# Two attention layers on one core: group totals in pairs, differences of the next input on GpSimd, and broadcasts placed within the even steps

## The chip, the cores and the metric

The kernel runs on one core of a Trainium2 chip. The metric is device time in microseconds, the median of several runs. The time before is 3956.3 us (three runs, 3953.38 to 3957.62).

A core has five engines with a queue each: TensorE (PE, matrix products), VectorE (DVE), ScalarE (ACT), GpSimd (POOL) and SyncE (SP, which here only issues DMAs; GpSimd issues some too). Each engine works its queue in order, and waits for the others by semaphores.

## The reference, cut to what matters

The input x has 8 images of 512 channels and 32 x 32 = 1024 positions. Two layers follow one another, both with 8 heads of 64 channels, all in float32:

```python
# layer 0, on gn(x): group norm, then plain attention
weight = softmax(einsum('bct,bcs->bts', q * s, k * s))      # 1024 x 1024 for each head
a = einsum('bts,bcs->bct', weight, v)
x = x + einsum('oc,bct->bot', proj_w, xf + a) + proj_b
# layer 1, on gn(x): attention with mixed heads, and an instance norm of the weights
attn = einsum('bhdq,bhdT->bhqT', q, k) * scale
attn = softmax(einsum('gh,bhqT->bgqT', w_head, attn))
attn = (attn - mean) / sqrt(var + EPS) * in_gamma + in_beta  # over each head's 1024 x 1024
out = einsum('bhqT,bhdT->bhqd', attn, v) @ w_proj.T + b_proj
x = x + out
```

What matters here: both softmaxes are left undivided until after the product with v. The kernel forms exponentials, sums of them (the totals), reciprocals of the totals, and multiplies the attention's output with the reciprocals, which it must first spread over the partitions by way of DRAM.

## The kernel before

**Projections.** Every 512 x 512 projection is a 2 x 2 block product by 7 products instead of 8 (Winograd's form of Strassen). It needs sums and differences of the four quarters of the right-hand side: `combine_right` forms four differences, each of 128 x 1024 elements, the second from the first and the fourth from the second. `ORDER = (1, 6, 2, 7, 5, 3, 4)` is one order of the products. Product 6 needs the second difference, product 7 the third, product 5 the first and product 4 the fourth; 1, 2 and 3 need none.

**Layer 0, attention** (`attention0`, once per batch). The work is 64 pieces, i = 0 to 63, eight per group g; a group is a pair of heads and half of the positions. `scores(i)` makes 1024 scores per partition on PE and exponentials on ACT; `values(i)` multiplies them with v on PE; `sums(i)` adds the exponentials into `zacc[g]` on DVE. The loop takes two pieces at a time, with values two pieces behind the scores. What else is due stands in an agenda by slot (a value of i): with i the end of a group, `totals(g)` at i + 2, `reciprocals(g)` at i + 6, `finish(g)` at i + 10.

- `totals(g)`: four small matmuls with a matrix of ones sum `zacc[g]` over the partitions into a PSUM tile z, 256 columns in each of four 32-row strips. ACT copies it to `row`, SP stores it into `zc[g]` by DMA as 128 x 8.
- `reciprocals(g)`: DVE adds the two halves of the output, takes the reciprocal, SP writes it to DRAM (`zd`) and reads it back spread over 64 partitions, twice (`rzb[g]`); two small checks follow on DVE.
- `finish(g)`: DVE multiplies the output with `rzb[g]` and adds it into `xa`.

What is due after slot 65 runs in a flush, `ag.flush()`, that stands behind the next batch's first projection (`qk0`, or `first_q1` after the last batch) and before its second (`v0`, or `first_k1`). During the attention the agenda also holds the statistics of the next batch (`stats0`: slots 20 to 47, with two small matmuls pm and pv at slots 43 and 45 that PE executes in order between its pieces) and loads: `load_left("k")` at 32, `load_left("v")` at 33, 1792 KB each.

**Layer 1, attention** (`Attention1`, once per batch). The positions of the queries are taken in 8 chunks p, with each step in four quarters t. Chunk p's scores are made in step p, moved by DMA so that a head lies on its own partitions (`regroup`, `re<-raw`), mixed over the heads on PE and exponentiated on ACT in step p + 1 (`mix`), transposed on DVE (`flip`), measured on DVE (`moments`, the BN statistics), and multiplied with v in steps p + 1 and p + 2 (`values`). Step 8 has no new chunk: it is the turn, where the first projection of the next batch (`k_projection`, its right-hand side the next input y) is woven in. `right_tile` takes a tile from the pool of the raw scores, `right_y` fills it with the four differences of y, and `k_go(1)`, `(2)`, `(6)`, `(7)`, later `(5)` and `(4, 3)`, are the products. Each product's result leaves PSUM by `leave`, on DVE or ACT, and the PSUM pool has three such tiles, shared with the scores and the mix.

Two chunks make a pair n. `totals(n)` stands in the second quarter of the odd steps (p = 3, 5, 7): DVE takes reciprocals, GpSimd writes them to DRAM in four DMAs (`zd<-rz`) and reads them back spread over 64 partitions each, in two DMAs (`rzb<-zd`, `broadcast(0)` and `broadcast(1)`), and `divide` on GpSimd multiplies the output with them (`q<-q,rzb`) in the last quarter of the even steps. The last pair of a batch does the same after step 8 on SP and DVE.

**What sets the order.** No scheduler reorders anything: each engine's queue holds its instructions in the order in which the program text emits them, by the steps and the agendas. A tile's pool hands out its buffers in that order too, and an instruction waits where its buffer is still in use.

Of the kernel before, what the change touches and what calls it, by code (L numbers as in the profile page):

```python
# [9 lines left out]
F32 = mybir.dt.float32  # L10
# [8 lines left out]
P = 128  # L19
# [448 lines left out]
def tile_two_attention_layers(  # L468
# [19 lines left out]
    nc = tc.nc  # L488
    B, C, T = x_d.shape
# [3 lines left out]
    NT = T // P  # L493
    FB = 512
# [206 lines left out]
    with ExitStack() as l0:  # L701
# [49 lines left out]
        def load_blocks(which, queue=nc.sync, tag="u0"):  # L751

            t = left_tile(which, 0)
            if tag == "junk":
                a21[which] = zpool.tile([P, T], F32, tag=tag, name=f"a21_{which}", bufs=1)[
                    :, :C
                ].rearrange("p (k o) -> p k o", k=2)
            else:
                a21[which] = zpool.tile([P, 2, HC], F32, tag=tag, name=f"a21_{which}")
            for dst, i, j in (  # L760
                (t[:, 0], 0, 0), (t[:, 1], 0, 1), (a21[which], 1, 0), (t[:, 2], 1, 1),
            ):
                for k in range(2):
                    queue.dma_start(
                        out=dst[:, k],
                        in_=SOURCES[which][ts(2 * j + k, P), i * HC : (i + 1) * HC],
                    )
# [308 lines left out]
        def attention0(b, agenda):  # L1076
# [18 lines left out]
            def sums(i):  # L1095
                g, kc = i // NG, i % NG
                if kc == 1:
                    zacc[g] = zpool.tile([P, 2, FB], F32, tag="zacc", name=f"zacc_{b}_{g}")
                    nc.vector.tensor_add(zacc[g], e[i - 1], e[i])  # L1099
                elif kc > 1:  # L1100
                    nc.vector.tensor_add(zacc[g], zacc[g], e[i])  # L1101

            def values(i):

                g, hp, kc = i // NG, i // NG % (H // 2), i % NG
                if kc == 0:
                    acc[g] = [
                        ps_a.tile([P, FB], F32, tag=f"a{a}", name=f"a0_{b}_{g}_{a}", bufs=2 - a)
                        for a in range(2)
                    ]  # L1110
                for a in range(2):
                    rows = slice(a * D, a * D + D)
                    for m in range(2):
                        nc.tensor.matmul(  # L1114
                            acc[g][a][m * D : m * D + D], v[rows, kc, ts(2 * hp + m, D)],
                            e[i][rows, m], start=(kc == 0), stop=(kc == NG - 1),
                        )
                if kc == NG - 1:

                    u[g] = [  # L1120
                        zpool.tile([P, FB], F32, tag=f"u{a}", name=f"u_{b}_{g}_{a}")
                        for a in range(2)
                    ]
                    for a in (1, 0):
                        nc.scalar.copy(u[g][a], acc[g][a])

            def totals(g):


                HB = FB // 2  # L1130
                z = ps_a.tile([P, FB], F32, tag="a0", name=f"z_{b}_{g}", bufs=2)[:, :HB]
                for c in range(4):
                    nc.tensor.matmul(
                        z[c * 32 : c * 32 + 32], ones[:, :32], zacc[g][:, c // 2, ts(c % 2, HB)],
                        start=True, stop=True, tile_position=(0, c * 32),
                    )
                row = zpool.tile([P, HB], F32, tag="row", name=f"row0_{b}_{g}")
                nc.scalar.copy(row, z)
                zc[g] = stat.tile([P, T // P], F32, tag="zc", name=f"zc_{b}_{g}")
                nc.sync.dma_start(out=zc[g], in_=row[0::32])  # L1140

            def reciprocals(g):

# [22 lines left out]
            def finish(g):  # L1166
                hp, f = g % (H // 2), g // (H // 2)
                nc.vector.tensor_mul(u[g][0], u[g][0], rzb[g])
                dst = xa_t[b][:, hp, ts(f, FB)]
                nc.vector.tensor_add(dst, dst, u[g][0])  # L1170


            for i in range(0, NI + 2, 2):
                if i < NI:
                    scores(i)
                    scores(i + 1)
                if i >= 2:
                    for w in (i - 2, i - 1):
                        values(w)
                        sums(w)  # L1180
                    if (i - 1) % NG == NG - 1:
                        g = (i - 1) // NG
                        agenda.at(i + 2, lambda g=g: totals(g))
                        agenda.at(i + 6, lambda g=g: reciprocals(g))
                        agenda.at(i + 10, lambda g=g: finish(g))
                agenda.run(i)
                agenda.run(i + 1)

# [82 lines left out]
    with ExitStack() as l1:  # L1271
# [78 lines left out]
        def quarters(n):  # L1350
            return [[n[:, 2 * i : 2 * i + 2, ts(j, FB)] for j in range(2)] for i in range(2)]

        def combine_right(t, n, parts=range(4)):

            (b11, b12), (b21, b22) = quarters(n)
            for i in parts:
                x, y = ((b12, b11), (b22, t[:, 0]), (b22, b12), (b21, t[:, 1]))[i]
                nc.vector.tensor_sub(t[:, i], x, y)  # L1358

        class Projection:  # L1360
            ORDER = (1, 6, 2, 7, 5, 3, 4)
# [63 lines left out]
            t = rawpool.tile([P, H * FB], F32, tag="raw", name=f"left_p_{b}")  # L1425
            load_left(("p", b), t[:, : 14 * HC])

        def right_y(b, parts=range(4)):
            combine_right(right_t[b], y_t[b], parts)

        def k_projection(b):
            t = k_t[b] = shared.tile([P, NCC, T], F32, tag="k", name=f"k1_{b}")
# [192 lines left out]
        class Attention1:  # L1625
# [140 lines left out]
            def totals(self, n):  # L1766

                b, last = self.b, n == NCH - 1
                bn = self.stats(n)
                del self.bn[n]  # L1770
                ps = acc_psum(f"z1_{b}_{n}")
                nc.tensor.matmul(ps[:64, :32], bn[:, :, 1], sel256, start=True, stop=True)
                for i, x in enumerate((bn[:, :, 2], self.sq)):
                    nc.tensor.matmul(ps[:64, 32:64], x, sel, start=(i == 0), stop=(i == 1))
                rz = stat.tile([64, 32], F32, tag="rz", name=f"rz1_{b}_{n}")
                nc.vector.reciprocal(rz, ps[:64, :32])  # L1776
                nc.vector.tensor_copy(self.zs[:, n], ps[:64, :64])
                zd = dram.tile([2, H, P], F32, tag=f"zd_{b}_{n}", name=f"zd_{b}_{n}")
                queue = nc.sync if last else nc.gpsimd
                for r in range(2):  # L1780
                    for t in range(2):
                        queue.dma_start(  # L1782
                            out=zd[t].rearrange("g (r c q) -> r c g q", r=2, q=4)[r],
                            in_=rz[32 * t + r : 32 * t + 32 : 2].rearrange("c (g q) -> c g q", q=4),
                        )
                self.rzb = zpool.tile([P, T], F32, tag="rzb", name=f"rzb_{b}_{n}")
                self.zd, self.zq = zd, queue
                self.broadcast(0)

            def broadcast(self, t):  # L1790

                self.zq.dma_start(
                    out=self.rzb[t * D : t * D + D],
                    in_=self.zd[t].rearrange("g i -> (g i)").partition_broadcast(D),
                )
# [70 lines left out]
            def step(self, p, t, ag):  # L1866

                new, old, older = p < NT, p >= 1, p >= 2
                if t == 0:
# [10 lines left out]
                    if old:  # L1880
                        self.mix(p - 1, 0)
                    ag.run(4 * p - 0.25)
                elif t == 1:
                    if older:
                        self.values(p - 2, 1, 0)
                        self.flip(p - 1, 0)
                        if p % 2:
                            self.totals(p // 2 - 1)
                        elif p >= 4:
                            self.broadcast(1)  # L1890
                        self.moments(p - 1, 0)
                    if new:
                        self.scores(p, 3)
# [2 lines left out]
                    if old:  # L1896
                        self.mix(p - 1, 1)
                elif t == 2:
                    if older:
                        self.values(p - 2, 1, 1)  # L1900
                    if new:
# [63 lines left out]
        for b in range(B):  # L1965
# [11 lines left out]
            if more:  # L1977
# [14 lines left out]
                kp = []  # L1992
                ag.at(4 * NT - 0.5, lambda: right_tile(b + 1))
                ag.at(4 * NT - 0.5, lambda: k_go(1))
                ag.at(4 * NT, lambda: right_y(b + 1, [0, 1]))
                ag.at(4 * NT + 0.5, lambda: k_go(2))
                ag.at(4 * NT + 1, lambda: right_y(b + 1, [2, 3]))
                ag.at(4 * NT + 1, lambda: left_p(b))
                ag.at(4 * NT + 1.5, lambda: k_go(6))
                ag.at(4 * NT + 2.5, lambda: k_go(7))  # L2000
# [16 lines left out]
            if not more:  # L2017
                a.values(last, 0, 2, 3)
                a.leave(last, 0)
                out_products[0](0, [2])  # L2020
                out_products[0](1, [0, 1])
                a.values(last, 1, 0, 1, 2, 3)
                a.leave(last, 1)
                a.totals(NCH - 1)
                a.broadcast(1)
                a.instance()
                out_products[1]()
                continue
# [4 lines left out]
            a.values(last, 1, 0, 1, 2, 3)  # L2033
            a.leave(last, 1)
            a.totals(NCH - 1)
            a.broadcast(1)
            a.instance()
            k_leave()
# [72 lines left out]
```

## Time and profile before

| what | us |
|---|---|
| median of three runs | 3956.3 |
| the profiled execution's own time | 3957.8 |
| its span, first to last instruction | 3956.0 |
| PE busy in it | 3873.6 |
| the four small matmuls of totals in layer 0, L1133, all 64 groups | 40.9 |
| the copy of z on ACT, L1138, 64 of 0.37 | 23.8 |
| differences of y on DVE, L1358 `right`, 28 of 1.21 (median) | 33.8 |
| product with the reciprocals on GpSimd, L1819, 24 | 56.5 |

The granted TensorE clock was 0.999 over the whole span.

The sums of busy time are of overlapping pieces. A group's line in the profile gives line, engine, operation, output and input tiles with their shapes, how many, and then busy us and mean ns of one, and the idle time of the engine before them with what ended it. These are the two largest groups, one of layer 1 on DVE and one of layer 0 on PE:

```profile
L1704 DVE STREAM_TRANSPOSE et<-e 128x2048 f32<-128x2048 f32 x256 | 589.4, 2302 | 100.4 <-ACT e L1689 99.2
...
L1088 PE MATMUL s<-q,k 64*64 64x512 f32 x4096 | 490.1, 593 | 2.3 <-ACT e L1093 2.3
```

PE matmuls overlap, so that 593 ns is the length of one and not the distance to the next. A float32 matmul leaves two records. In the order of time, a line has the start, the length of the merged piece, the engine, the source line, the operation and, in brackets, the idle time before it and what released it.

### The profile page before, as it was taken

To read this page: it belongs to the slowest core of one execution; us is meant where nothing else is said; L and a number is where in the kernel's file an instruction comes from. 1 tells how busy PE (TensorE), PEld (TensorE's weight loads), DVE (VectorE), ACT (ScalarE), POOL (GpSimd) and SP (SyncE) were. 2 spreads that over 40 slices of the span, in tenths; PEclk is the share of its full clock that TensorE was granted. 3 is DMA by queue.
4 is the path that set the end of the run, shared out by engine and by line. 5 is a ranking of instruction groups with operands and counts; after the bars stand their busy time and mean duration, and the time that the engine had idled before them with its cause. 6 is when DMAs were issued, how large, how long until landed. Compare 5 with 4: busy or idle time off the path is not lost. (4 is left out here: it accounts for less than half of the span.)

```text
span 3956.0 us, 95453 instructions
## 1 busy us (share of the span) xinstructions
PE 3873.6 (98%) x41868; PEld 1820.5 (46%) x41868; DVE 2770.1 (70%) x3741; ACT 1970.7 (50%) x2432; POOL 140.9 (4%) x182
## 2 busy tenths in 40 slices
PE   8999999999999999999999999999999999999998
PEld 4353534344353535344544544545545445445454
DVE  4747475665758474756967958859768769678597
ACT  1726354453627172534816717538347257176274
POOL 0000000000000000000100100001001001001010
PEclk9999999999999999999999999999999999999999
DMA  3313131121122121216938839749558479297495
GB/s 120 123 49 116 49 118 38 63 69 68 55 72 68 62 76 49 86 46 170 233 120 202 217 100 236 191 125 241 161 148 220 144 178 237 83 231 197 117 226 143
DMA packets 249593, 519.09 MB, mean 131 GB/s; under 512 B 51024, under 2 KB 58192, under 8 KB 242512
## 3 DMA queue, kind: packets, MB, share of 16 engines
q1 hardware_dynamic: 241984, 500.08, 44.6%
q0 software_dynamic: 7184, 12.81, 1.6%
q8 instruction: 331, 5.42, 0.6%
q14 instruction: 94, 0.77, 0.1%
HBM read 197.16 MB, written 46.92 MB: 62 GB/s over the span
## 5 line engine op out<-in xcount | busy, mean ns | idle before, releaser
L1704 DVE STREAM_TRANSPOSE et<-e 128x2048 f32<-128x2048 f32 x256 | 589.4, 2302 | 100.4 <-ACT e L1689 99.2
L1734 PEld LDWEIGHTS a<-et,v 128*64 128x64 f32 x16384 | 506.0, 138 | 290.7 <-issue 263.6
L1718 DVE BATCH_NORM_STATS2 bn<-e 128x6 f32<-128x512 f32 x1024 | 634.9, 680 | 0.0
L1093 ACT ACTIVATE e<-s 128x1024 f32<-128x1024 f32 x512 | 497.2, 1026 | 234.2 <-PE s L1088 233.8
L1651 ACT COPY raw<-s 128x1024 f32<-128x1024 f32 x480 | 470.2, 1018 | 214.3 <-PE s L1639 189.6
L1689 ACT ACTIVATE e<-m 128x1024 f32<-128x1024 f32 x512 | 496.2, 1021 | 156.7 <-PE m L1676 54.9
L1734 PE MATMUL a<-et,v 128*64 128x64 f32 x16384 | 553.8, 224 | 6.1 <-issue 3.5
L1101 DVE TENSOR_TENSOR zacc<-zacc,e 128x1024 f32<-128x1024 f32 x384 | 468.7, 1221 | 88.4 <-ACT e L1093 66.3
L1639 PE MATMUL s<-k,q 64*64 64x512 f32 x4096 | 514.6, 606 | 5.9 <-DVE q L1498 3.2
L1088 PE MATMUL s<-q,k 64*64 64x512 f32 x4096 | 490.1, 593 | 2.3 <-ACT e L1093 2.3
L1114 PE MATMUL a<-e,v 64*64 64x512 f32 x4096 | 484.0, 589 | 0.0
L1676 PE MATMUL m<-re,wmix 32*32 32x512 f32 x8192 | 312.5, 599 | 19.6 <-DMA re<-raw 16.1
L1114 PEld LDWEIGHTS a<-e,v 64*64 64x64 f32 x4096 | 156.7, 133 | 282.8 <-issue 282.5
L1088 PEld LDWEIGHTS s<-q,k 64*64 64x64 f32 x4096 | 147.9, 133 | 275.1 <-issue 240.7
L1639 PEld LDWEIGHTS s<-k,q 64*64 64x64 f32 x4096 | 128.1, 132 | 220.6 <-issue 87.8
L1458 PE MATMUL pv<-wv,y 128*128 128x512 f32 x480 | 214.3, 599 | 0.0
L1782 POOL DMA_DIRECT2D zd<-rz x96 | 52.3, 550 | 3507.7 <-DVE rz L1776 3505.6
L1750 ACT COPY q<-a 64x256 f32<-64x256 f32 x256 | 93.9, 367 | 145.8 <-PE a L1734 144.2
L1676 PEld LDWEIGHTS m<-re,wmix 32*32 32x32 f32 x8192 | 69.3, 103 | 165.0 <-ACT raw L1651 74.6
L1458 PEld LDWEIGHTS pv<-wv,y 128*128 128x128 f32 x480 | 88.6, 190 | 119.8 <-issue 106.5
L1464 DVE COPY v<-pv 128x512 f32<-128x512 f32 x30 | 20.7, 689 | 159.6 <-PE pv L1458 81.0
L1099 DVE TENSOR_TENSOR zacc<-e,e 128x1024 f32<-128x1024 f32 x64 | 78.3, 1223 | 55.4 <-ACT e L1093 55.4
(318 smaller groups left out, 3871.0 us busy)
## 6 DMA issues: line engine op xcount, KB each, us to landing
re<-raw SPq DMA_DIRECT2D x1024, 256.0 KB
left_q<-left_q SPq DMA_DIRECT2D x17, 1792.0 KB
left_p<-left_p SPq DMA_DIRECT2D x17, 1792.0 KB
left_k<-left_k SPq DMA_DIRECT2D x10, 1792.0 KB
x<-in_x_dram SPq DMA_DIRECT2D x32, 512.0 KB
rzb<-zd SPq DMA_DIRECT2D x128, 128.0 KB
x<-x SPq DMA_DIRECT2D x64, 256.0 KB
y<-x SPq DMA_DIRECT2D x32, 512.0 KB
```

The source lines that it names most:

```text
L1088: nc.tensor.matmul(ps[c * D : c * D + D, m], k[r, hp, k0 : k0 + D], q[r, hp, ts(f, FB)], start=True, stop=True,)
L1093: nc.scalar.activation(e[i], ps, AF.Exp, scale=S0 * S0)
L1101: nc.vector.tensor_add(zacc[g], zacc[g], e[i])
L1114: nc.tensor.matmul(acc[g][a][m * D : m * D + D], v[rows, kc, ts(2 * hp + m, D)], e[i][rows, m], start=(kc == 0), stop=(kc == NG - 1),)
L1458: nc.tensor.matmul(ps[:, m], y_t[b][:, c, ts(2 * i + m, P)], w[:, c], start=(c == 0), stop=(c == NCC - 1),)
L1639: nc.tensor.matmul(ps[c * D : c * D + D, m], qo_t[b][r, p, hp, ts(c, D)], k_t[b][r, hp, ts(kh, FB)], start=True, stop=True,)
L1651: nc.scalar.copy(dst, ps)
L1676: nc.tensor.matmul(ps[a // 2][c * 32 : c * 32 + 32, a % 2].rearrange("p (r h k) -> p h r k", r=2, h=2), wmix[rows].rearrange("p g i -> p ( ...
L1689: nc.scalar.activation(e[:, :, 2 * h : 2 * h + 2].rearrange("p r a k -> p a r k"), ps[h].rearrange("p a (r k) -> p a r k", r=2), AF.Exp,)
L1704: nc.vector.transpose(self.et[p, u].rearrange("p kb (r st a) g q -> p st kb r (a g q)", r=2, st=2)[:, st], self.e[p, s].rearrange("p r a ( ...
L1718: nc.vector.bn_stats(self.bn[n][:, p % 2, s, a], e[:, :, a].rearrange("p r k -> p k r"))
L1734: nc.tensor.matmul(acc[two * D : two * D + D, s].rearrange("p (x q) -> p x q", q=4), v_t[b][:, kb, ts(g, D)], et[:, kb, :, g], start=(kb = ...
```

## The change

It has three parts.

1. **Layer 0.** `totals(g)` is called for odd g alone and handles g - 1 and g: eight small matmuls into one PSUM tile of 512 columns, one copy of 512 columns on ACT, two DMAs into `zc`. Its slot, two after the odd group's end, stays; `reciprocals` of both groups follow in one slot (i + 6), and `finish` of the two at i + 10 and i + 12. To hold two groups, `zacc`, the first half of the output `u0` and the tile `a21` that shares its tag get three buffers instead of two, `zc` four, and `row` one of double width.
2. **Layer 1, the turn.** `right_y` forms all four differences on GpSimd at one place, in the first quarter of step 8 before the mix, right after `right_tile`; before, DVE formed two at the end of the first quarter and two at the end of the second. `combine_right` gets the engine as an argument; the other call, for the output's projection, stays on DVE.
3. **Layer 1, broadcasts.** `totals(n)` no longer calls `broadcast(0)`. Both broadcasts stand in the even steps, the first at the end of the first quarter's mix, the second at the start of the third quarter; after step 8 they are called explicitly for the last pair, in the order as before. The tile `rzb` is taken when the first broadcast is issued.

```diff
             def totals(g):
                 HB = FB // 2
-                z = ps_a.tile([P, FB], F32, tag="a0", name=f"z_{b}_{g}", bufs=2)[:, :HB]
-                for c in range(4):
-                    nc.tensor.matmul(
-                        z[c * 32 : c * 32 + 32], ones[:, :32], zacc[g][:, c // 2, ts(c % 2, HB)],
-                        start=True, stop=True, tile_position=(0, c * 32),
+                z = ps_a.tile([P, FB], F32, tag="a0", name=f"z_{b}_{g}", bufs=2)
+                for i in range(2):
+                    for c in range(4):
+                        nc.tensor.matmul(
+                            z[c * 32 : c * 32 + 32, ts(i, HB)], ones[:, :32],
+                            zacc[g - 1 + i][:, c // 2, ts(c % 2, HB)],
+                            start=True, stop=True, tile_position=(0, c * 32),
+                        )
+                row = zpool.tile([P, FB], F32, tag="row", name=f"row0_{b}_{g}", bufs=1)
+                nc.scalar.copy(row, z)
+                for i in range(2):
+                    t = zc[g - 1 + i] = stat.tile(
+                        [P, T // P], F32, tag="zc", name=f"zc_{b}_{g - 1 + i}", bufs=4
                     )
-                row = zpool.tile([P, HB], F32, tag="row", name=f"row0_{b}_{g}")
-                nc.scalar.copy(row, z)
-                zc[g] = stat.tile([P, T // P], F32, tag="zc", name=f"zc_{b}_{g}")
-                nc.sync.dma_start(out=zc[g], in_=row[0::32])
+                    nc.sync.dma_start(out=t, in_=row[0::32, ts(i, HB)])
...
                         g = (i - 1) // NG
-                        agenda.at(i + 2, lambda g=g: totals(g))
-                        agenda.at(i + 6, lambda g=g: reciprocals(g))
-                        agenda.at(i + 10, lambda g=g: finish(g))
+                        if g % 2:
+                            agenda.at(i + 2, lambda g=g: totals(g))
+                            for j in range(2):
+                                agenda.at(i + 6, lambda g=g - 1 + j: reciprocals(g))
+                                agenda.at(i + 10 + 2 * j, lambda g=g - 1 + j: finish(g))
...
-        def right_y(b, parts=range(4)):
-            combine_right(right_t[b], y_t[b], parts)
+        def right_y(b):
+            combine_right(right_t[b], y_t[b], nc.gpsimd)
...
-                self.rzb = zpool.tile([P, T], F32, tag="rzb", name=f"rzb_{b}_{n}")
-                self.zd, self.zq = zd, queue
-                self.broadcast(0)
+                self.zd, self.zq, self.zn = zd, queue, n
 
             def broadcast(self, t):
 
+                if t == 0:
+                    self.rzb = zpool.tile(
+                        [P, T], F32, tag="rzb", name=f"rzb_{self.b}_{self.zn}"
+                    )
...
                     ag.run(4 * p - 0.25)
+                    if p % 2 == 0 and p >= 4:
+                        self.broadcast(0)
                 elif t == 1:
...
                         if p % 2:
                             self.totals(p // 2 - 1)
-                        elif p >= 4:
-                            self.broadcast(1)
...
                 elif t == 2:
+                    if p % 2 == 0 and p >= 4:
+                        self.broadcast(1)
...
                 ag.at(4 * NT - 0.5, lambda: right_tile(b + 1))
                 ag.at(4 * NT - 0.5, lambda: k_go(1))
-                ag.at(4 * NT, lambda: right_y(b + 1, [0, 1]))
+                ag.at(4 * NT - 0.5, lambda: right_y(b + 1))
                 ag.at(4 * NT + 0.5, lambda: k_go(2))
-                ag.at(4 * NT + 1, lambda: right_y(b + 1, [2, 3]))
```

More of the change, by code (lines that the diff above doesn't have):

```diff
@@ L758, in load_blocks @@
             else:
-                a21[which] = zpool.tile([P, 2, HC], F32, tag=tag, name=f"a21_{which}")
+                a21[which] = zpool.tile([P, 2, HC], F32, tag=tag, name=f"a21_{which}", bufs=3)
             for dst, i, j in (
@@ L1097, in sums @@
                 if kc == 1:
-                    zacc[g] = zpool.tile([P, 2, FB], F32, tag="zacc", name=f"zacc_{b}_{g}")
+                    zacc[g] = zpool.tile(
+                        [P, 2, FB], F32, tag="zacc", name=f"zacc_{b}_{g}", bufs=3
+                    )
                     nc.vector.tensor_add(zacc[g], e[i - 1], e[i])
@@ L1120, in values @@
                     u[g] = [
-                        zpool.tile([P, FB], F32, tag=f"u{a}", name=f"u_{b}_{g}_{a}")
+                        zpool.tile([P, FB], F32, tag=f"u{a}", name=f"u_{b}_{g}_{a}", bufs=3 - a)
                         for a in range(2)
@@ L1351, in quarters, with combine_right @@
             return [[n[:, 2 * i : 2 * i + 2, ts(j, FB)] for j in range(2)] for i in range(2)]
-        def combine_right(t, n, parts=range(4)):
+        def combine_right(t, n, engine=nc.vector):
             (b11, b12), (b21, b22) = quarters(n)
-            for i in parts:
+            for i in range(4):
                 x, y = ((b12, b11), (b22, t[:, 0]), (b22, b12), (b21, t[:, 1]))[i]
-                nc.vector.tensor_sub(t[:, i], x, y)
+                engine.tensor_sub(t[:, i], x, y)
         class Projection:
@@ L1785, in totals @@
                         )
-                self.rzb = zpool.tile([P, T], F32, tag="rzb", name=f"rzb_{b}_{n}")
-                self.zd, self.zq = zd, queue
-                self.broadcast(0)
+                self.zd, self.zq, self.zn = zd, queue, n
             def broadcast(self, t):
+                if t == 0:
+                    self.rzb = zpool.tile(
+                        [P, T], F32, tag="rzb", name=f"rzb_{self.b}_{self.zn}"
+                    )
                 self.zq.dma_start(
@@ L2024, in tile_two_attention_layers @@
                 a.totals(NCH - 1)
+                a.broadcast(0)
                 a.broadcast(1)
@@ L2035, in tile_two_attention_layers @@
             a.totals(NCH - 1)
+            a.broadcast(0)
             a.broadcast(1)
```

## The prediction

> **What bounds the kernel.** I read the page first, then what TensorE (PE) waits for, then the order of time at the places the diff touches.
>
> ```profile
> PE 3873.6 (98%) x41868; PEld 1820.5 (46%) x41868; DVE 2770.1 (70%) x3741; ACT 1970.7 (50%) x2432; POOL 140.9 (4%) x182
> ...
> PE pk L1383 <- DVE re L1400: 8.2, 7, 1.2
> ...
> PE pk L1383 <- DVE right L1358: 2.6, 7, 0.4
> ```
>
> The columns of a wait are total us, times, longest. PE is hardly ever idle, so the time falls by PE work taken out plus PE waits taken out; nothing else counts. Two of these waits come exactly 7 times, once for each turn from one batch to the next in layer 1.
>
> **Part 1, totals of two groups together.** PE in layer 0, in order of time:
>
> ```profile
> 1410.36 1.90 PE L1088 MATMUL s<-q,k 64*64 64x512 f32 x16
> 1412.08 1.90 PE L1114 MATMUL a<-e,v 64*64 64x512 f32 x16
> 1413.90 0.64 PE L1133 MATMUL z<-zacc,ones 128*32 128x256 f32 x8
> 1414.47 1.95 PE L1088 MATMUL s<-q,k 64*64 64x512 f32 x16
> 1416.24 1.90 PE L1114 MATMUL a<-e,v 64*64 64x512 f32 x16
> ```
>
> Without a z, pieces start every 1.72 us. From a (1412.08) to the next a (1416.24) is 4.16 us where two pieces are 3.43: a visit of z costs 0.73 us. What would a second group in the same visit cost? A 16-record piece is two rounds of four tiles side by side over 512 columns in 1.72, so 0.86 a round; z has 256 columns, so 0.43 (estimate). At worst it costs the 0.64 that the row shows as its whole span. I take 0.43, since nothing changes between the two rounds.
>
> Per batch there are 7 visits in the loop and one in the flush after it. Afterwards 3 remain in the loop and 1 in the flush, each with two groups. Removed: 4 x 0.73 = 2.92, but in 7 batches one removed z shares its visit with the small matmul pm of the statistics (z to pm takes 0.57), so there 2.75. Added: 3 x 0.43 = 1.29. In the flush PE now waits 0.28 for DVE after z (pv_p started 236.97, k ended 236.92), so the added 0.43 costs only 0.15. Sum: 7 x (2.75 - 1.29 - 0.15) + 1 x (2.92 - 1.44) = **10.7 us less**. At 0.64 for the second group it would be some 4.
>
> The copies on ACT (64 of 0.37 become 32 of about 0.58) and the same DVE work in other slots lie beside PE. Two places are near the edge. The flush before, SP's broadcast and then DVE:
>
> ```profile
> 240.65 1.10 SPq L1152 DMA_DIRECT2D rzb<-zd  x2
> ...
> 244.40 0.69 DVE L1168 TENSOR_TENSOR u<-u,rzb 128x512 f32<-128x512 f32 x1 [4.98 <-DMA rzb<-zd]
> ...
> 247.71 1.22 DVE L935 TENSOR_TENSOR tmp<-tmp,pv_p 128x1024 f32<-128x1024 f32 x1 [1.89 <-PE pv_p L906]
> ```
>
> DVE stands still until the broadcast lands, and behind it waits L935, which frees a PSUM tile for PE's product 7. With z at T = 236.06 (SP issued zc at 237.16 and zd at 239.24): the second group's write to DRAM queues on SP behind the first group's broadcast, which itself waits for the first write. First reciprocal about T+3.7, its broadcast issued T+5.3, second write T+6.5, second broadcast T+7.9 to T+9.0, landed T+11.6 (2.6 after the issue, as here), finished T+13.0. L935 then starts at T+13.0 where it was ready at T+11.8; product 7 needs it done by T+15.2, and it is done at T+14.2. One us is left; I cost it at nothing. The loads of left_q behind it go out 3 us later, with some 16 us to their use.
>
> The other place is slot 44: finish of the even+1 group now stands before the statistics' squares, 1.33 us of DVE ahead of a PE matmul. In three of seven batches DVE had 2.5 us to spare there (gs_sq ended 1.38, pv at 3.91 after pm at 815.61), in the batch of 1458.42 only 0.9. But those late ones came from a reciprocal held up by the 3.6 MB of left_k and left_v (a wait of 0.7 to 1.7 us on them). These loads follow the odd group's broadcast in SP's new order and can go some 5 slots earlier, ahead of the next totals. Nothing, at worst 3 us.
>
> **Part 2, the differences on GpSimd.** DVE at a turn (statistics L1718 just before, until 3364.94), then PE:
>
> ```profile
> 3364.86 1.20 DVE L1358 TENSOR_TENSOR right<-y 128x1024 f32<-128x1024 f32 x1
> 3365.98 1.22 DVE L1358 TENSOR_TENSOR right<-y,right 128x1024 f32<-128x1024 f32 x1
> 3367.12 1.21 DVE L1398 TENSOR_TENSOR re<-re,pk 128x1024 f32<-128x1024 f32 x1
> ...
> 3366.21 3.67 PE L1383 MATMUL pk<-right,left_k 128*128 128x512 f32 x8 [0.37 <-DVE right L1358]
> ...
> 3374.14 3.70 PE L1383 MATMUL pk<-right,left_k 128*128 128x512 f32 x8 [1.17 <-DVE re L1400]
> ```
>
> Product 7 waits 0.37 for the third difference; product 5 waits 1.17 for a PSUM tile that L1400 frees at 3374.08. Take the four differences from DVE: L1398 starts at 3364.9, flip 3366.1, statistics to 3370.9, L1400 done at 3372.1. PE, 0.37 earlier, asks at 3372.6. Both waits go: 7 x 1.54 = **10.8 us**. What is late next: the flip of the last quarter, done at 3375.0, needed at about 3378.
>
> Can GpSimd deliver? Its queue around the turn:
>
> ```profile
> 3335.12 2.18 POOL L1782 DMA_DIRECT2D zd<-rz  x4 [26.87 <-DVE rz L1776]
> 3341.41 1.06 POOL L1792 DMA_DIRECT2D rzb<-zd  x2 [4.11 <-DMA zd<-rz]
> 3349.09 2.34 POOL L1819 TENSOR_TENSOR q<-q,rzb 128x1024 f32<-128x1024 f32 x1 [6.63 <-DMA rzb<-zd]
> ```
>
> The differences come right behind zd and wait only for the old raw tile to be read out by the regroup DMAs, about 3346 to 3348. At 2.35 each (the product of the same shape) the second is done near 3353, needed at 3359.05 by product 6; all at 3357.5. Six us to spare.
>
> Here two rules of the Trainium skill speak against the change. GPSIMD Engine Reference, Engine selection, sends elementwise work to VectorE since GpSimd takes about twice as long. The rows agree (2.35 against 1.21), and if instruction time decided, 7 x 4 x 1.14 = 32 us would be lost; but GpSimd is 4% busy and DVE stands in PE's way, so the wait rows decide. SBUF — State Buffer, Who interferes with whom, says that the two share a port under an exclusive lock. This trace shows it: one difference took 2.52 us instead of 1.21 (2798.43) beside a GpSimd product begun at 2797.51. Were all DVE work locked out for 9.4 us, L1400 would come some 2.8 us later than now and layer 1 lose 7 x 2.5 = 17 us. But the page limits it to DVE work with two SBUF inputs or in a two-port mode, and the statistics beside that GpSimd product (3348.80) took 2.47 for four, as elsewhere. Between 3342 and 3366 DVE has only flips and statistics, one input each. I take no loss.
>
> **Part 3, the broadcasts.** GpSimd runs far ahead of the program's steps: it held zd, rzb, rzb, product in this order before, and for the first two pairs of a batch the order is the same after, so nothing moves. Only the third pair's broadcasts now fall behind the four differences, to about 3358, with the product at about 3365; its result is read after 3395. The 0.5 MB then no longer run beside the regroup DMAs that PE waits for at that point (L1676 waits 16.1 us for them in all, of which here 0.22, 1.58 and 0.51 us in three turns). I take 1.5 us less; bounds 0 and 2.3.
>
> **Sum.** 10.7 + 10.8 + 1.5 = 23 us. From the profiled execution (span 3956.0, time 3957.8) that gives 3934.8. It was 1.5 above the median 3956.3, so against the median: **3933.5 us**, 0.6% faster.
>
> **Rivals.**
> (a) Only layer 0 pays: another wait (ACT's exponentials, DVE's next flip) takes the place of the two. For it: the turn is a tight weave, margins of 0.5 us. Against it: each step above has slack. 3956.3 - 10.7 = 3945.6.
> (b) Only layer 1 pays: the second group costs its full 0.64 and DVE's squares and the flush take back the remaining 4. 3956.3 - 12.3 = 3944.
> (c) Slower: the doubled chain in the flush. The longest wait of SP for a zd write was 3.6 us instead of the 1.1 in the flush; twice this makes the second broadcast land 5 us later, one us of it is slack, and PE stalls 4 us in each of 8 batches: 3933.5 + 32 = 3965. It decides from 1.0 us of delay on; slower than before from 3.9. Against it: those 3.6 us came beside large loads, and none is in flight in the flush.
> (d) The change does less than it says: GpSimd's differences start late behind something I did not see, PE waits as before, and the flush eats layer 0: about 3956.
>
> **Chances.** Main case 0.68 (3926 to 3941), (a) 0.10, (b) 0.10, (c) 0.06, (d) 0.06. The range reaches to (a) and (b): 3925 to 3948. No change means within 0.2%, 8 us, about what a measurement of this kernel can tell. Faster 0.88, same 0.06, slower 0.06.
>
> **What would show it.** Layer 0: the period of a pair of groups falls from 28.93 (2 x 14.46) to about 28.6. Layer 1: the waits on L1358 and L1400 gone from PE's list, four POOL differences of about 2.35 between zd and rzb, done before product 6. Wrong if PE waits in v0's product 7 on L935, if pv in the statistics waits for gs_sq, or if DVE flips beside the differences are longer than 2.3.

## The result, and the profile after

| | before | after |
|---|---|---|
| median (us) | 3956.96 (6 runs, 3948.13 to 3959.82) | 3937.57 (6 runs, 3935.46 to 3948.04) |
| ratio, 95% interval | | 0.9959, 0.9944 to 0.9974 |
| profiled execution: time, span | 3957.8, 3956.0 | 3948.0, 3946.2 |

The change makes the kernel faster. The ratio puts the gain at 16 us (0.0041 x 3956), the two medians at 19.4. The profiled execution is the slowest of its six, so its span shows less of the gain than the median. First the busy line of the page after, then what PE waits for (total us, times, longest):

```profile
PE 3871.6 (98%) x41868; PEld 1822.3 (46%) x41868; DVE 2736.6 (69%) x3713; ACT 1966.8 (50%) x2400; POOL 207.4 (5%) x210
```

```profile
PE m L1684 <- DMA re<-raw: 14.4, 17, 1.9
...
PE a L1742 <- issue: 6.2, 5, 2.5
...
PE pv_p L906 <- DVE tmp L935: 3.3, 5, 1.7
...
PE pk L1391 <- DVE re L1406: 2.8, 7, 0.6
```

34 us of differences moved from DVE to GpSimd (twice as long there: 67). The two waits of exactly 7 times, on `right` and on the tile that L1400 freed, are gone. Two others have come: one on L1406, again once for each turn, and one on L935 in the flush of layer 0, which the list of before does not have. They are what separates the result from the forecast.

A total over a layer hides this, so I cut PE's order of time into stages and compared sums. Each number is the time between the first PE instruction of one stage and the first of the next, in the profiled execution of each kernel (the last three columns are experiments below):

| stage, us | before | after | after, again | differences alone | writes first |
|---|---|---|---|---|---|
| layer 0 attention, 8 loops | 932.8 | 921.9 | 922.3 | 932.2 | 922.0 |
| `v0`, the product behind the flush, 8 | 194.1 | 199.3 | 200.8 | 194.1 | 194.1 |
| layer 1 turns, 7 | 406.6 | 395.3 | 395.3 | 395.0 | 395.3 |
| rest of layer 1 attention, with the projections next to it | 1557.2 | 1565.7 | 1559.4 | 1550.8 | 1554.2 |

The last row is the trap of this profile. After shows 8.5 us more there, in waits for the regroup DMAs and in "issue" that come at no fixed place. The same kernel, profiled again, shows 6 less. This row swings by 15 us between kernels whose code for it is nearly the same. Some 3 us of that are the clock (estimate, half of each spell): in this stretch the granted clock falls to 0.5 for 3.41 us once in before and in "writes first", twice in each profile of after, and never in "differences alone". The first three rows repeat to 1.5 us and carry the comparison.

**Layer 0's loop.** PE in the order of time, after:

```profile
340.37 1.90 PE L1116 MATMUL a<-e,v 64*64 64x512 f32 x16
342.19 1.07 PE L1135 MATMUL z<-zacc,ones 128*32 128x256 f32 x16
343.19 1.95 PE L1088 MATMUL s<-q,k 64*64 64x512 f32 x16
...
370.82 1.07 PE L1135 MATMUL z<-zacc,ones 128*32 128x256 f32 x16
```

Two groups in one visit take 1.07, where one took 0.64: the second costs 0.43. From one visit to the next it is 370.82 - 342.19 = 28.63, for the two periods of 14.46 before.

**The turn.** GpSimd's queue at the turn of 3342, then PE's, and the line of DVE that PE waits for:

```profile
3341.93 2.44 POOL L1366 TENSOR_TENSOR right<-y 128x1024 f32<-128x1024 f32 x1 [9.08 <-ACT e L1697]
3344.45 2.39 POOL L1366 TENSOR_TENSOR right<-y,right 128x1024 f32<-128x1024 f32 x1
...
3349.19 2.40 POOL L1366 TENSOR_TENSOR right<-y,right 128x1024 f32<-128x1024 f32 x1
3351.52 1.06 POOL L1802 DMA_DIRECT2D rzb<-zd  x2
```

```profile
3354.01 3.70 PE L1391 MATMUL pk<-right,left_k 128*128 128x512 f32 x8
...
3361.16 3.24 PE L1391 MATMUL pk<-right,left_k 128*128 128x512 f32 x7 [0.36 <-DVE re L1406]
```

```profile
3359.81 1.20 DVE L1406 TENSOR_TENSOR re<-re,pk 128x1024 f32<-128x1024 f32 x1
```

The second difference ends at 3346.8, and product 6 wants it at 3354.0; all four are done by 3351.6. Product 7 still waits 0.36, no longer for its operand but for L1406 on DVE (3359.81 to 3361.01), which adds product 6 to a sum and so frees the PSUM tile of product 6. This wait is new and was not hidden before: there product 7 began at 3366.21 and the addition of product 6 (L1398) at 3367.12, after it. So it is in all seven turns of the three kernels with the differences on DVE (product 7 begins 2.12 us before that addition ends), and in none of the seven profiles with them on GpSimd. That the pool now hands product 7 the tile of product 6 is what this suggests; why it does, with no edit to these tiles, no run shows.

**The flush.** SP's queue after the end of a batch whose z started at 1301.77, then DVE and PE:

```profile
1303.51 1.19 SPq L1146 DMA_DIRECT2D zc<-row  x2
1305.59 0.32 SPq L1155 DMA_DIRECT2D zd<-rz  x1
1308.82 1.14 SPq L1158 DMA_DIRECT2D rzb<-zd  x2
1310.01 0.58 SPq L1155 DMA_DIRECT2D zd<-rz  x1
1312.43 1.08 SPq L1158 DMA_DIRECT2D rzb<-zd  x2
```

```profile
1315.92 0.69 DVE L1174 TENSOR_TENSOR u<-u,rzb 128x512 f32<-128x512 f32 x1 [2.20 <-DMA rzb<-zd]
1316.65 0.69 DVE L1176 TENSOR_TENSOR xa<-xa,u 128x512 f32<-128x512 f32 x1
1317.26 1.21 DVE L935 TENSOR_TENSOR tmp<-tmp,pv_p 128x1024 f32<-128x1024 f32 x1
```

```profile
1318.53 3.72 PE L906 MATMUL pv_p<-left_v,tmp 128*128 128x256 f32 x16 [1.68 <-DVE tmp L935]
```

The chain reads off directly. Both reciprocals began within a microsecond of each other (1305.36 and 1306.29 on DVE), but the second write stands behind the first broadcast on SP, which waits until the first write has landed (here 3.2 after its issue). Then the second broadcast waits 2.4 for the second write. It lands at 1315.9, DVE comes to L935 at 1317.3, and PE, which had run out of work at 1316.85, has stood 1.68. It lost a little more than that: this `v0` took 26.22 for the 24.28 of before, 1.94.

### The profile page after: what moved, and what is told of

The parts are those of the page before. It is cut to its first block, busy times and chain, and to the rows that moved or that the text cites. A ratio compares the mean times of both kernels' runs of the same rounds, so it can differ in the third digit from the quotient of the medians.

```text
span 3946.2 us, 95344 instructions
## 1 busy us (share of the span) xinstructions
PE 3871.6 (98%) x41868; PEld 1822.3 (46%) x41868; DVE 2736.6 (69%) x3713; ACT 1966.8 (50%) x2400; POOL 207.4 (5%) x210
## 5 line engine op out<-in xcount | busy, mean ns | idle before, releaser
L906 PE MATMUL pv_p<-left_v,tmp 128*128 128x256 f32 x512 | 115.0, 380 | 3.3 <-DVE tmp L935 3.3
```

## Experiments

Each ran beside the kernel before on the same chip. The first four ran in one set, with the median of before at 3955.83 (27 runs); so did the last four, with 3955.81 (34 runs).

**1. The changed kernel again**, to tell what of its first profile is chance.

> The changed kernel once more, to separate what repeats from what doesn't. In its first profile layer 1 outside the turns took 8.5 us longer than before (two attention stages by 6.4 and 5.1 us, waits of PE on the regroup DMAs and on nothing visible), though nothing was changed there. Theory: this is chance of one execution; in a new profile these stages lie within 3 us of before in sum, the turns again gain 1.2 to 3 us each, and the stretch of v0 again loses 4 to 6 us in sum. Time about 19 us under before (ratio 0.995). Rival: the moved broadcasts and the work on GpSimd disturb the regroup DMAs; then the same stages are again 5 to 10 us longer and the time is 10 us under before.

Measured: 3941.3 (5 runs, 3936.94 to 3947.56), ratio 0.9961 (0.9947 to 0.9974). The stage table has it: loops, `v0` and turns repeat, the 8.5 us in layer 1 do not. The wait on L935 came again (3.8 us in 3 batches, longest 2.7), and that on L1406 with the same 2.8 in 7. The longest, in the flush of the sixth batch, cost twice. PE:

```profile
1319.22 5.41 PE L906 MATMUL pv_p<-left_v,tmp 128*128 128x256 f32 x16 [2.74 <-DVE tmp L935]
```

Product 7 itself took 5.41 where it took 3.72 above, with a granted clock of 0.68 from 1319.2 to 1324.6. Behind the wait of 1.68 in the first profile the clock stayed at 1.00. This is why the sum of `v0` is 200.8 here.

**2. Part 1 alone**: the totals of two groups together; GpSimd gets no differences and the broadcasts stay.

> Only the totals of two groups together; differences on VectorE and broadcasts as before. Theory: the loop gains 1.26 to 1.5 us per batch, 10.9 in all, and the flush gives back 5 to 6 since PE's product 7 in v0 waits for VectorE, which waits for the second broadcast: 5 us under before (ratio 0.9987). Rival: the loss in v0 is not of this part (VectorE is late for another reason); then 11 us under before and no wait on the L935 line.

Measured: 3951.04 (21 runs), ratio 0.9990 (0.9983 to 0.9997). Its stages: loops 922.0 (10.8 less than before), `v0` 198.2 (4.1 more), turns 405.9 as before. Almost half of what the loop gains is given back in the flush. Its list has the wait on L935 and both old waits of the turn.

**3. The differences on GpSimd alone**, with the broadcasts at their old places in the program. `right_y` and `combine_right` are those of the changed kernel.

```diff
-                ag.at(4 * NT, lambda: right_y(b + 1, [0, 1]))
+                ag.at(4 * NT - 0.5, lambda: right_y(b + 1))
                 ag.at(4 * NT + 0.5, lambda: k_go(2))
-                ag.at(4 * NT + 1, lambda: right_y(b + 1, [2, 3]))
```

> Only the four differences on GpSimd; totals one by one, first broadcast at the odd step as before. Theory: each of the 7 turns gains 1.2 us, as in the changed kernel (0.37 of the wait of product 7 stays, on the addition that frees its tile): 8.5 us, and up to 2.3 more where the regroup DMAs were waited for at a turn; 9 to 11 us under before (ratio 0.9975). The first half of the third pair's broadcast is now ahead of the differences in GpSimd's queue, the second behind them. Rival: work on GpSimd locks VectorE out of its port, flips and statistics beside it get longer than 2.31 and 0.68 us each, and the gain is under 4 us.

Measured: 3943.59 (7 runs), ratio 0.9970 (0.9959 to 0.9982). The turns come to 395.0: all that the full change gains there. The medians of 2 and 3 add up to 4.8 + 12.2 = 17.0 us less than before, about the gain of the whole.

**4. Part 1 and the rest, with both writes ahead of both broadcasts.** `reciprocals(g)` keeps its write, and the two reads back move into a function that the agenda calls after both:

```diff
                 nc.sync.dma_start(out=zd, in_=rz)
-                rzb[g] = zpool.tile([P, FB], F32, tag="rzb", name=f"rzb_{b}_{g}")
-                for m in range(2):
-                    nc.sync.dma_start(...)
+                zds[g] = zd
...
+            def spread(g):      # the rzb tile and the two broadcasts, from zds[g]
...
+                            for j in range(2):
+                                agenda.at(i + 6, lambda g=g - 1 + j: spread(g))
```

> The changed kernel, with both groups' writes to DRAM put ahead of both broadcasts on the SP queue. Theory: the second write no longer queues behind the first broadcast (which waits for the first write), the second broadcast is issued about T+6.5 instead of T+8.9 after z at T, lands about T+10, and VectorE reaches the L935 line when its product is done, near T+11.8, instead of T+13.5 to T+15.5. The waits of product 7 on L935 go: 5 us under the changed kernel, 24 under before (ratio 0.994). Rival: the landing of the second broadcast is bound by the DMAs themselves (a read of 64 partitions that takes 2.6 us whatever stands ahead, or DRAM latency that grows with two writes in flight); then v0 still loses 3 us or more.

Measured: 3934.46 (5 runs, 3932.31 to 3936.78), ratio 0.9947 (0.9934 to 0.9961). SP's queue in the same batch's flush, whose z started at 1299.51, then PE:

```profile
1301.26 1.20 SPq L1146 DMA_DIRECT2D zc<-row  x2
1303.34 1.25 SPq L1155 DMA_DIRECT2D zd<-rz  x2
1306.34 2.41 SPq L1171 DMA_DIRECT2D rzb<-zd  x4
```

```profile
1299.51 1.07 PE L1135 MATMUL z<-zacc,ones 128*32 128x256 f32 x16
1300.51 7.17 PE L906 MATMUL pv_p<-left_v,n 128*128 128x256 f32 x32
1307.52 10.53 PE L906 MATMUL pv_p<-left_v,tmp 128*128 128x256 f32 x48
```

The second write now flies beside the first. The last of the four broadcasts is issued by 9.2 after z (1306.34 + 2.41), where it took until 11.7 in the batch shown above; L935 started at 1312.79, 13.3 after z instead of 15.5, and product 7 runs into its predecessors without a gap (x48 in one piece). `v0` is back at 194.1, to 0.01 us the sum of before, and no wait on L935 is left. This shows the cause of the 5.2 us: the order on SP, not the second group's bytes and not the doubled DVE work, which are the same here.

**5. The same, and DVE's order at the turn changed**: in step 8 the statistics of the second quarter stand behind the leave of product 6, so that L1406 (L1411 in this kernel) comes some 2 us earlier.

```diff
                     k_leave()
+                    if not new:
+                        self.moments(p - 1, 1)
...
                     self.flip(p - 1, t)
-                    self.moments(p - 1, t)
+                    if new or t != 1:
+                        self.moments(p - 1, t)
```

> Writes first, as before, and in step 8 VectorE adds product 6 (which frees its PSUM tile) ahead of the statistics of the second quarter instead of behind them. Theory: what PE's product 7 still waits for at each turn, 0.36 us, is the PSUM tile of product 6; with the addition moved ahead of 2.4 us of statistics this wait goes, 7 x 0.36 = 2.5 us under writes_first (ratio to before 0.994), if the statistics, now later, don't hold up the last exponentials, which need their buffer. Rival: product 7 waits for a VectorE semaphore that comes with later work, or the statistics' delay makes PE wait at product 5 instead: no gain, or 2 us lost.

Measured: 3932.6 (5 runs, 3930.35 to 3936.09), ratio 0.9940 (0.9927 to 0.9954). In the order of time of PE, product 7 now has no bracket:

```profile
3341.05 1.14 PE L1689 MATMUL m<-re,wmix 32*32 32x512 f32 x32
3342.12 2.08 PE L1747 MATMUL a<-et,v 128*64 128x64 f32 x64
3344.14 3.70 PE L1396 MATMUL pk<-right,left_k 128*128 128x512 f32 x8
```

Every turn takes 56.03 (before: 57.67 to 59.48), in sum 392.2, another 3.1 less than with experiment 4, about what the row on L1406 held. The two ratios' intervals overlap, so that the times alone do not tell kernels 4 and 5 apart; the trace does. This is the fastest version found, and faster than both kernels of the case: its slowest run (3936.1) is below every run of before and below the median of after.

**6. Part 3 alone**: the broadcasts moved, everything else as before.

> Only the broadcasts moved in the text; totals one by one, differences on VectorE. Theory: GpSimd's queue holds the same instructions in the same order as before, so nothing moves: time as before within 0.1%, turns of 57.7 to 59.5 us. Rival: the place in the text changes what the DMAs wait for, the regroup DMAs land earlier, and PE's 16 us of waits for them shrink by several us.

Measured: 3957.49 (13 runs), ratio 1.0001 (0.9991 to 1.0010). Turns 406.5, as before. GpSimd's queue holds zd, both broadcasts and the product in the old order, so nothing moves in time.

**7 and 8. The differences made two and three times over**, on GpSimd, everything else as after: does the work on GpSimd slow DVE by the shared port, and how much room was there?

```diff
-                engine.tensor_sub(t[:, i], x, y)
+                for _ in range(times):
+                    engine.tensor_sub(t[:, i], x, y)
```

> The changed kernel with each of the four differences computed twice in a row on GpSimd (same result). Theory: the second one was done at 3346.8 + 0 in the profile of the changed kernel where product 6 begins at 3354.0; twice the work ends it near 3351.6, the third near 3356.4 for product 7 at 3360.8: still in time, turns stay at 56.43 us and the time at that of the changed kernel. Flips and statistics of VectorE beside 19 us of GpSimd work stay at 2.30 and 0.68 us. Rival (the port lock): more GpSimd work beside VectorE lengthens these, and the turns by 1 us or more.

> The same with each difference computed three times. Theory: now the second one ends near 3356.4 by the same clock, 2.4 us after product 6 wants to begin: PE waits there, turns take 58.5 to 59.3 us instead of 56.43, 15 to 20 us over the changed kernel in 7 turns. If it costs nothing either, the slack is larger than I read; if it costs more than 30 us, the lock or GpSimd's start counts.

Measured: twice 3939.84 (13 runs), ratio 0.9963 (0.9953 to 0.9974); three times 3959.02 (12 runs), ratio 1.0002 (0.9992 to 1.0011). With two of each, GpSimd is at it for 19.6 us at a turn, and the turns still come to 395.4. DVE in that stretch (differences on GpSimd from 3334.89 to 3354.52):

```profile
3342.46 2.31 DVE L1713 STREAM_TRANSPOSE et<-e 128x2048 f32<-128x2048 f32 x1 [2.53 <-ACT e L1698]
3344.70 2.52 DVE L1727 BATCH_NORM_STATS2 bn<-e 128x6 f32<-128x512 f32 x4
...
3352.92 1.20 DVE L1407 TENSOR_TENSOR re<-re,pk 128x1024 f32<-128x1024 f32 x1
```

All three have nearly their usual lengths. Those that lie wholly beside the differences, against the others of the same trace: a flip 2306 ns (2302), a statistic 689 (680), that is 1%, where the clash in the trace before doubled an instruction. With three of each the second difference comes too late. PE's waits of that kernel:

```profile
PE pk L1392 <- POOL right L1367: 16.1, 12, 2.8
```

The turns grow to 412.4, by 17.1. The row makes up 16.1, and the 2.8 on L1406 are gone; in two of the turns the granted clock falls to 0.5 for 3.41 us behind such a wait (2812.5, 3089.0), which costs some 1.7 each (estimate). So GpSimd's time costs nothing up to twice the work, and what exceeds the room is paid in full, with the clock on top. The room ahead of product 6 is 3354.0 - 3346.8 = 7.2 us in the turn shown of after (the forecast had six): doubling puts the second difference 4.9 later, tripling 9.8. A shared port would have shown as longer DVE rows and slower turns with two already.

## Why the prediction was right and where it failed

The stage sums close the account. After against before: loop -10.9, the products ahead of the flush +0.6 (25.23 for 25.14, seven times), `v0` +5.2, turns -11.3, together **-16.4**; the ratio gives -16. For experiment 4 it is -10.8 + 0.6 + 0.0 - 11.3 = -21.5, and the medians differ by 21.4. The forecast was -23.

- **The loop: right, 8% too large.** A visit's second group cost 0.43 as taken, and the pair's period is 28.63 for 28.6 forecast. Working out the loop alone from the prediction's terms, 7 x (2.75 - 1.29) + (2.92 - 1.29) = 11.9, and 10.9 came. Two of the four visits taken out of a batch, those of its first and its seventh group, save 0.63 and not 0.73: the scores at their place take 2.00 instead of 1.90 (at 415.19, after). That is 1.5 us in 15 places. ACT has no idle time just ahead (412.00 to 416.05 there), so PE may wait for its exponentials; this was not tested. Against it, the wait of 0.5 for pm at 1458.42 in before is gone.
- **The flush: the step that failed.** "One us is left; I cost it at nothing." Its first half was exact: first reciprocal forecast at T+3.7 and found at T+3.6, first broadcast T+5.3 and typically T+5.2, second write T+6.5 and T+6.4. Then I let the second write land 1.4 after its issue, as a write alone does, and put the second broadcast at T+7.9. It was issued at T+8.9 as a rule: with the first broadcast's 2 x 128 KB just ahead of it the write took 2.5. In the flush of the sixth batch the first write was late too, 2.9 to 3.6 in all seven profiles with the totals in pairs, and in none of the three without; why stays open. L935 started at T+13.8 to T+15.5, not T+13.0. The deadline was wrong as well. In each of the seven flushes of after, `v0` grew by the time from T+14.76 to the end of L935: 0.27 for an end at T+15.03, 0.99 for T+15.75, 1.94 for T+16.70. In experiment 4 an end at T+14.5 cost nothing. So behind the forecast's T+14.2 there was half a microsecond and not one, and the second broadcast alone was one late. The sum is 5.2, of which the wait row shows 3.3; some 0.27 in each of the seven stands in no bracket. It is the mechanism of rival (c), which I priced from a delay of 5 us and gave 0.06; it came at a sixth of its price. "It decides from 1.0 us of delay on" should have been 0.5. A margin as large as the spread of the latency that it is made of is no cover.
- **The copies, the squares at slot 44, the loads: right.** No wait for gs_sq appeared in the loop; the loads of left_k and left_v did go out earlier (357.2 instead of 368.8 in the second batch).
- **The turn: size right, parts not.** 12.3 were forecast with part 3, 11.3 came. Both waits went, and GpSimd delivered by 3351.6 in the turn shown. But I had product 7 running on the moment `right` was early. It now waits for L1406, by 0.36 to 0.6 us, 2.8 in all, a dependence that the kernel before does not have; I had asked what else comes late, and not whether the edit gives an instruction something new to wait for. Against that, the irregular part of the turns of before went too: what they had above their floor of 57.67, 2.9 us in sum.
- **Part 3: its 1.5 us were credited to the wrong edit.** Moved alone, the broadcasts do nothing (1.0001). The third pair's broadcasts are late because the four differences stand before them on GpSimd. With the differences on GpSimd and the old places (experiment 3), only the second broadcast falls behind them, and the turns are as short. In the turns, none of the seven profiles with the differences on GpSimd has a wait for the regroup DMAs; the three without have two or three each (2.3 us in before, 1.5 in experiment 2, 2.1 in experiment 6). Whether the delayed half of the broadcasts or the changed order on DVE removes them was not tried, and stays open.
- **The port: right.** The trace before had it at its worst (2.52 for 1.21, one difference with two inputs in SBUF). The Trainium skill, SBUF — State Buffer, "Who interferes with whom", restricts it to DVE work with two SBUF inputs or in a two-port mode, and experiment 7 agrees: flips, statistics and a sum of one SBUF and one PSUM operand kept their lengths within 1.3% beside 19.6 us of GpSimd. The change even removes the clash, since the differences that suffered are now themselves on GpSimd. The rule of the GPSIMD Engine Reference, "Engine selection", against elementwise work there holds for the length of an instruction (2.4 against 1.21) and would have cost this kernel 12 us.

## What to carry to other kernels

When two short chains of write, wait, read back go over one queue, issue both writes before the first read: the order "write, read, write, read" makes the second write wait for the first one's landing, and cost 5 us here, half of what the pairing gained. Behind an edit, an instruction can wait for something that it did not need before: read in the trace after what each waits for anew, and not only whether the old waits have gone. Measure a margin against the time from which lateness really costs, which here was 0.3 us earlier than the end of PE's last row. In a trace of which one stage swings by 15 us from execution to execution, compare stage by stage, and believe a difference only where it repeats.

## What the runs showed that I had not expected

- A 4 KB write to DRAM, issued right behind a broadcast of 2 x 128 KB on the same queue, let its reader go 2.5 us after its issue; alone 1.4. In the sixth flush a write with no broadcast before it took 2.9 to 3.6, in every profile with the totals in pairs.
- PE stood 0.3 to 1.9 us longer in `v0` where the wait rows show 3.3 of 5.2 us. A list of waits gives a lower bound for what a late operand costs.
- After the two longest waits for L935 (2.74 in experiment 1, 2.16 in the last experiment) the granted clock was 0.5 for 3.41 us, and product 7 took 5.41 instead of 3.72. After 1.68 it was not.
